# Loading the range flag into the engines' registers inside layer 1 of a two-layer graph kernel

## The chip, the cores and the metric

The kernel runs on one core of one Trainium2 chip. The metric is the device time of one execution in microseconds (us), lower is better. The core has five engines that run their own instruction queues: TensorE (PE in the profile, its weight loads apart as PEld), VectorE (DVE), ScalarE (ACT), GpSimd (POOL) and SyncE (SP, which here only issues DMAs).

## The reference

There are 3327 nodes with 64 features each, and a dense 3327 x 3327 adjacency matrix of zeros and ones. Two layers are added to `x`, each on `h = relu(layernorm(x))`. Cut to what matters:

```python
# layer 0: hyperbolic attention over the neighbours
c = 1.0 / r[0] ** 2
x_t = logmap0(h, c)
adj_att = sigmoid(left[:, None] + right[None, :] + b_att[0]) * adj    # left, right: x_t @ halves of w_att
x_local = logmap(h[:, None, :], h[None, :, :], c)                     # one vector per pair of nodes
support_t = einsum('ij,ijd->id', adj_att, x_local)
x = x + proj(expmap(h, support_t, c), c)
# layer 1: the last 100 neighbours of each row, weights halved from the last one backwards
mask = (adj != 0); rank = cumsum(mask, axis=1); deg = rank[:, -1:]
k = minimum(deg, 100); pos = rank - (deg - k)
w = mask * where(pos > 0, 0.5 ** (k - pos), 0.0)
x = x + w @ (relu(layernorm(x)) @ weight) + bias
```

## The kernel before

The nodes are padded to 26 blocks of 128. The program has two versions of the whole computation. `fast` (line 447) uses approximations that hold when the inputs lie in a certain range; while it runs it works out a one-element integer tile `flag` that is 0 when they do (`in_range`, lines 963 to 980, written by VectorE at line 979). `general` (line 86) computes the same without that assumption. `gnn_kernel` runs `fast`, loads `flag` into a register of each of the five engines (`values_load`, line 1367), and each engine branches on it (line 1368): `general` runs, and overwrites the output, only if the flag is above 0. For the inputs here it is 0, so every engine jumps over `general`'s instructions to the end of the program.

`fast` handles layer 0 in four strips of columns (8, 8, 6 and 4 blocks), each against all 26 row blocks in rounds. On the way it leaves, for each pair of nodes, a byte that says how many neighbours lie behind (`behind`), from which layer 1's weights are decoded. After a strip its per-node work (`post`, lines 992 to 1150) turns the sums into the new `x` and into `s2`, layer 1's input in two half-precision parts (written by ScalarE at line 1147 and by VectorE at line 1149).

Layer 1 starts at line 1271. It is a sum over the 26 row blocks: for a block `j`, `decode(j)` makes a weight tile `wt` of 128 x 3328, in turn on ScalarE (line 1285) and on VectorE (line 1287), and `add(j, wt, n)` (line 1299) multiplies `s2` of that block with one chunk of 512 columns, into one of seven accumulators `pw`. The loop over `order` does this for blocks 0 to 21. The last strip's blocks, 22 to 25 (`late` = 22 onwards), come after it, since their `s2` is ready only when the last strip's per-node work has ended. They are added chunk by chunk: the four late blocks into chunk `n`, then a copy of the accumulator to `ow` (lines 1340 and 1342, ScalarE and VectorE in turn), then, two chunks later, `close`: small matmuls with the layer's weight matrix (line 1328), the sum with `x_sb` on VectorE (line 1330), and the output DMA on SP (line 1332; the ragged end of the last block goes from ScalarE's queue, line 1334).

The order on TensorE, VectorE and ScalarE is the order of the source:

```python
IN_ORDER = {mybir.EngineType.PE, mybir.EngineType.DVE, mybir.EngineType.Activation}   # line 32
```

Layer 1 is recorded in `tc.manual_schedule(engines=IN_ORDER)` (line 1274). The instructions of POOL and SP are not in this set; the framework's scheduler sets their order. A weight load of TensorE is an instruction of its own ahead of its matmul, and carries the wait for `s2`.

Of the kernel before, what the change touches and what calls it, by code (L numbers as in the profile page):

```python
# [446 lines left out]
def fast(ctx, tc, x, adj_t, r, w_att, b_att, weight, bias, out, flag):  # L447

    nc = tc.nc
# [95 lines left out]
    def behind(j):  # L545
        if j in JD:
            return weight_of[:, j - JD.start]
        return behind_of["lo"][:, j] if j < JD.start else behind_hi[:, j - JD.stop]
# [619 lines left out]
    def per_node(k, pa):  # L1168
        nb = STRIPS[k][1]
        agg = post_pool.tile([P, nb, D + 1], F32, name="agg_last" if k + 1 == len(STRIPS) else "agg")  # L1170
        for c in range(0, nb, 4):
            m = min(4, nb - c)
            to, of = agg[:, c : c + m], pa[:, c * P : c * P + m * (D + 1)].rearrange("p (b d) -> p b d", b=m)
            if c == 0:
                V.tensor_copy(to, of)
            else:
                A.copy(to, of)
        return post(agg, k)
# [5 lines left out]
    def advance(portions):  # L1184
        for stage in stages:
            while portions > 0 and not stage.asked:
                portion = next(stage.portions, LATER)
                stage.asked = portion == ACT
                if portion >= LATER:
                    break  # L1190
                portions -= portion

    def asked_of_act():
        for stage in stages:
            if stage.asked:
                next(stage.portions)
                stage.asked = False

    def finish():
        for stage in stages:  # L1200
            for _ in stage.portions:
                pass
        stages.clear()
# [70 lines left out]
    with tc.tile_pool(name="l1", bufs=2, reuse_waits="tile") as l1, tc.manual_schedule(engines=IN_ORDER):  # L1274
        decoded = 0

        def decode(j):

            nonlocal decoded
            if j in JD:  # L1280
                return behind(j)
            wt = l1.tile([P, NP], U16, name="wt", bufs=7)
            decoded += 1
            if decoded % 2:
                A.activation(wt, behind(j), AF.Copy, scale=128.0)
            else:
                V.tensor_scalar(wt, behind(j), 128.0, None, op0=ALU.mult)  # L1287
            return wt

        every = [*order, *range(late, NB)]  # L1290
        weights = {j: decode(j) for j in every[: len(JD) + 1]}
        stages.append(Stage(per_node(len(STRIPS) - 1, pa)))
        sums.close()
        l1_ps = ctx.enter_context(tc.tile_pool(name="l1_ps", bufs=1, space=PSUM, reuse_waits="tile"))
        pw = [l1_ps.tile([P, f1 - f0], F32, name=f"pw{n}") for n, (f0, f1) in enumerate(chunks)]

        def add(j, wt, n):
            f0, f1 = chunks[n]
            T.matmul(pw[n], s2[:, j].rearrange("p c d -> p (c d)"), wt[:, f0:f1].bitcast(BF16),  # L1299
                     start=j == order[0], stop=j == NB - 1)  # L1300

        def bias(b0, nb):
            xb = x_sb[:, b0 : b0 + nb]
            G.tensor_add(xb, xb, bias_b[:, None, :].to_broadcast([P, nb, D]))  # L1304

        for i, j in enumerate(order):
            for jn in every[: i + 1 + LEAD]:
                if jn not in weights:
                    weights[jn] = decode(jn)
            asked_of_act()  # L1310
            advance(LAST)
            for n in range(len(chunks)):
                add(j, weights[j], n)
            if i % 4 == 3 and i < STRIPS[-2][0]:
                bias(i - 3, 4)
        finish()
        bias(STRIPS[-2][0], late - STRIPS[-2][0])
        bias(late, NB - late)
        for j in range(late, NB):
            if j not in weights:  # L1320
                weights[j] = decode(j)
        ow = [l1.tile([P, 512], F32, name="ow", bufs=4)[:, : f1 - f0] for f0, f1 in chunks]

        def close(n):
            f0, f1 = chunks[n]
            b0, nb = f0 // P, (f1 - f0) // P
            for b in range(nb):
                T.matmul(pw[n][:, b * D : (b + 1) * D], ow[n][:, b * P : (b + 1) * P], w2s, start=True, stop=True)
            o = l1.tile([P, 4, D], F32, name="o", bufs=4)
            V.tensor_add(o[:, :nb], pw[n][:, : nb * D].rearrange("p (b d) -> p b d", d=D), x_sb[:, b0 : b0 + nb])  # L1330
            full = nb if b0 + nb < NB else nb - 1
            nc.sync.dma_start(out[f0 : f0 + full * P, :].rearrange("(b p) d -> p b d", p=P), o[:, :full])
            if full < nb:
                nc.scalar.dma_start(out[f0 + full * P : N, :], o[: N - f0 - full * P, full])

        for n in range(len(chunks)):
            for j in range(late, NB):
                add(j, weights[j], n)
            if n % 2:
                A.copy(ow[n], pw[n])  # L1340
            else:
                V.tensor_copy(ow[n], pw[n])
            if n > 1:
                close(n - 2)
        close(len(chunks) - 2)
        close(len(chunks) - 1)


@with_exitstack
def gnn_kernel(  # L1350
    ctx: ExitStack,
    tc: tile.TileContext,
    x: bass.AP,
    adj_t: bass.AP,
    r: bass.AP,
    w_att: bass.AP,
    b_att: bass.AP,
    weight: bass.AP,
    bias: bass.AP,
    out: bass.AP,  # L1360
):
    keep = ctx.enter_context(tc.tile_pool(name="keep", bufs=1))
    flag = keep.tile([1, 1], I32, name="flag")
    args = (x, adj_t, r, w_att, b_att, weight, bias, out)
    with ExitStack() as inner:
        fast(inner, tc, *args, flag)
    cond = tc.nc.values_load(flag)
    with tc.If(cond > 0):
        with ExitStack() as inner:
            general(inner, tc, *args)  # L1370

# [27 lines left out]
```

## Time and profile before

| | |
|---|---|
| median of three runs | 416.37 us (414.42 to 418.77) |
| the profiled execution's own time | 418.25 us |
| its span (first to last instruction) | 416.4 us |
| VectorE, ScalarE, TensorE matmul busy | 90%, 88%, 87% |
| last computing instruction ends | 409.55 us after the span's start |

The profile is of one execution, and its times count from the first instruction. A line such as "L1299" is a line of the kernel before. A suffix q (SPq, DVEq) marks an engine's sequencer: register loads, branches, semaphore waits and DMA issues happen there and are not counted as the engine's busy time. In a timeline the first two numbers are start and duration, and the bracket at the end gives the idle time ahead of the instruction and what ended it.

### The profile page before, as it was taken

What the parts mean: (1) busy time and instruction counts of PE and PEld (TensorE: products, weight loads), DVE (VectorE), ACT (ScalarE), POOL (GpSimd) and SP (SyncE); (2) the same over time, 40 slices, a digit from 0 to 9 for tenths busy, and PEclk for the clock granted to TensorE, in tenths of its full rate; (3) what the DMA queues carried; (4) which work ended last, traced back from release to release, by engine and by line L of the source; (5) the groups of instructions that cost most, each with busy time, mean ns of one, the idle gap of its engine ahead of it and who ended that gap; (6) DMA issues with size and microseconds to landing.
All of it is one profiled execution on the core that took longest, in us unless ns stands there. A gap on an engine that the chain in (4) does not pass through costs nothing.

```text
span 416.4 us, 4699 instructions
## 1 busy us (share of the span) xinstructions
PE 361.1 (87%) x1436; PEld 154.4 (37%) x1460; DVE 373.1 (90%) x546; ACT 364.8 (88%) x411; POOL 124.0 (30%) x240
## 2 busy tenths in 40 slices
PE   0088999999997999999997999999777999899793
PEld 0063333333333333333333444444332333344352
DVE  4999799999999899999999798899989899898841
ACT  3589999999998899999999899999996999788810
POOL 8154200000000263930250163801405183452400
PEclk9998999999999899999999899999898999999987
DMA  7315544545466534554437255454643420000012
GB/s 218 123 40 143 161 148 147 158 145 161 146 186 181 152 107 148 153 151 109 145 113 178 94 153 151 119 146 128 186 117 104 114 87 0 2 0 0 2 25 65
DMA packets 23298, 48.99 MB, mean 118 GB/s; under 512 B 8789, under 2 KB 9245, under 8 KB 23265
## 3 DMA queue, kind: packets, MB, share of 16 engines
q1 hardware_dynamic: 20993, 47.66, 39.2%
q10 hardware_dynamic: 1808, 0.46, 0.6%
q0 software_dynamic: 464, 0.49, 0.5%
q8 instruction: 13, 0.21, 0.2%
q14 instruction: 20, 0.16, 0.1%
HBM read 46.40 MB, written 0.87 MB: 114 GB/s over the span
## 4 chain that ended last, share of the span: by engine, by line
DVE 33%; ACT 27%; PE 24%; issue 10%; POOL 3%; DMA 1%; DVEq 0%; POOLq 0%; ACTq 0%
DVE sg L663 9%; PE po L680 9%; ACT sg L653 8%; DVE sg L658 8%; ACT pq L857 8%; ACT pq L858 3%; DVE wt L1287 3%; PE pq L670 3%; PE pq L671 3%; DVE behind_lo L646 3%; PE pc L632 2%; PE pc L631 2%; ACT behind_lo L642 2%; ACT behind_hi L642 2%; PE pw L1299 2%
## 5 line engine op out<-in xcount | busy, mean ns | idle before, releaser
L680 PE MATMUL po<-sg,hw 128*65 128x512 f32 (+1 forms) x364 | 164.5, 576 | 0.5 <-DVE st L972 0.4
L663 DVE SCALAR_TENSOR_TENSOR sg<-pq,sg 128x1024 f32<-128x1024 f32 (+1 forms) x91 | 103.4, 1137 | 6.7 <-ACT pq L858 5.9
L658 DVE SCALAR_TENSOR_TENSOR sg<-sg,ad 128x1024 f32<-128x1024 f32 (+1 forms) x91 | 103.8, 1141 | 0.3
L653 ACT ACTIVATE sg<-left_b,right 128x1024 f32<-128x1024 f32 (+2 forms) x103 | 99.5, 979 | 0.0
L857 ACT ACTIVATE pq<-pq 128x1024 f32<-128x1024 f32 (+1 forms) x91 | 87.1, 957 | 3.5 <-PE pq L671 3.2
L858 ACT ACTIVATE pq<-pq 128x1024 f32<-128x1024 f32 (+1 forms) x91 | 86.2, 947 | 2.9
L680 PEld LDWEIGHTS po<-sg,hw 128*65 128x65 f32 x364 | 50.4, 141 | 71.3 <-issue 57.5
L631 PE MATMUL pc<-mask,ca 128*128 128x512 bf16 (+1 forms) x170 | 62.1, 365 | 11.1 <-DVE behind_hi L646 3.9
L670 PE MATMUL pq<-iu,ju 71*128 71x512 f16 (+1 forms) x182 | 68.2, 375 | 2.4 <-ACT jz L794 1.0
L671 PE MATMUL pq<-iz,jz 128*128 128x512 f16 (+1 forms) x182 | 67.2, 376 | 0.0
L632 PE MATMUL pc<-mask,cb 128*128 128x512 bf16 (+1 forms) x168 | 60.1, 368 | 2.2 <-ACT behind_lo L642 1.7
L620 DVE TENSOR_SCALAR mask<-ad 128x1024 bf16<-128x1024 f32 (+1 forms) x91 | 58.6, 645 | 0.0
L1044 POOL TENSOR_TENSOR dots<-dots,ih 128x8 f32<-128x8 f32 (+1 forms) x3 | 2.2, 720 | 134.3 <-DVE dots L1064 134.3
L1299 PE MATMUL pw<-wt,s 128*128 128x512 bf16 (+1 forms) x150 | 33.6, 374 | 4.3 <-DVE s L1149 2.2
L632 PEld LDWEIGHTS <-cb 128*128 128x128 bf16 x182 | 17.9, 98 | 51.7 <-issue 39.8
L631 PEld LDWEIGHTS <-ca 128*128 128x128 bf16 x175 | 17.3, 99 | 29.9 <-issue 17.8
L670 PEld LDWEIGHTS <-ju 71*128 71x128 f16 x182 | 18.1, 99 | 24.2 <-DVE sg L663 5.8
L1299 PEld LDWEIGHTS <-s 128*128 128x128 f16 x182 | 18.0, 100 | 23.6 <-issue 4.2
L642 ACT ACTIVATE behind_hi<-pc 128x1024 uint8<-128x1024 f32 (+2 forms) x25 | 21.8, 872 | 5.3 <-remote 3.3
L671 PEld LDWEIGHTS <-jz 128*128 128x128 f16 x182 | 18.2, 100 | 19.7 <-issue 3.3
L1304 POOL TENSOR_TENSOR x_sb<-x_sb,bias_b 128x256 f32<-128x256 f32 (+1 forms) x6 | 9.9, 1657 | 51.6 <-DVE w L1133 46.0
L642 ACT ACTIVATE behind_lo<-pc 128x1024 uint8<-128x1024 f32 (+2 forms) x29 | 24.9, 859 | 0.0
(313 smaller groups left out, 369.0 us busy)
## 6 DMA issues: line engine op xcount, KB each, us to landing
ad<-in_adj_t SPq DMA_DIRECT2D x65, 512.0 KB, 3.7
ad<-in_adj_t SPq DMA_DIRECT2D x26, 384.0 KB, 3.2
out<-o SPq DMA_DIRECT2D x6, 128.0 KB, 1.9
left_b<-left_d SPq DMA_DIRECT2D x1, 512.0 KB, 4.6
x_sb<-in_x ACTq DMA_DIRECT2D x1, 416.0 KB, 5.6
x_sb<-in_x SPq DMA_DIRECT2D x1, 416.0 KB
left_b<-left_d SPq DMA_DIRECT2D x1, 384.0 KB
jz<-iz POOLq DMA_DIRECT2D x2, 128.0 KB, 2.6
```

The source lines that it names most:

```text
L631: T.matmul(S.pc[:, f0:f1], ca, S.before[:, f0:f1], start=False, stop=True, skip_group_check=True)
L632: T.matmul(S.pc[:, f0:f1], cb, now[:, f0:f1], start=S.first, stop=True, skip_group_check=True)
L642: A.activation(kept, S.pc[:, : S.F], AF.Relu, scale=128.0 if j in JD else 1.0)
L653: A.activation(part(n, sg, j), S.left[:, : S.F], AF.Tanh, bias=right[:, j : j + 1], scale=0.5)
L658: V.scalar_tensor_tensor(sg, sg, 1.0, ad_of.pop(n)[:, :w], op0=ALU.add, op1=ALU.mult)
L663: V.scalar_tensor_tensor(sg, pq_of.pop(n)[:, :w], WD, sg, op0=ALU.add, op1=ALU.mult)
L670: T.matmul(part(n, pq, j, f0, f1), ju[:KB, j, :], S.iu[:, f0:f1], start=True, stop=False)
L671: T.matmul(part(n, pq, j, f0, f1), jz[:, j, :], S.iz[:, f0:f1], start=False, stop=True)
L680: T.matmul(S.po[: D + 1, f0:f1], hw[:, j, :], part(n, sg_of[n], j, f0, f1), start=j == NB - 1, stop=j == 0)
L857: A.activation(pq, pq, AF.Gelu, scale=-WG / QS)
L858: A.activation(pq, pq, AF.Gelu, scale=WH)
L1299: T.matmul(pw[n], s2[:, j].rearrange("p c d -> p (c d)"), wt[:, f0:f1].bitcast(BF16), start=j == order[0], stop=j == NB - 1)
```

## The change

The call that loads the flag into the registers moves from `gnn_kernel` into `fast`, ahead of the loop over the late blocks, and `fast` hands the loaded value back. The branch stays where it was.

```diff
@@ fast @@
             if full < nb:
                 nc.scalar.dma_start(out[f0 + full * P : N, :], o[: N - f0 - full * P, full])
 
+        general_too = nc.values_load(flag)
         for n in range(len(chunks)):
             for j in range(late, NB):
                 add(j, weights[j], n)
@@
         close(len(chunks) - 2)
         close(len(chunks) - 1)
+    return general_too
@@ gnn_kernel @@
     with ExitStack() as inner:
-        fast(inner, tc, *args, flag)
-    cond = tc.nc.values_load(flag)
-    with tc.If(cond > 0):
+        general_too = fast(inner, tc, *args, flag)
+    with tc.If(general_too > 0):
         with ExitStack() as inner:
             general(inner, tc, *args)
```

## The prediction

> **What bounds the kernel now.** I read the page's head first, then the chain that ended last, then the timeline around the place where the loads go, and last the flag's own line and the branch that follows it.
>
> ```profile
> PE 361.1 (87%) x1436; PEld 154.4 (37%) x1460; DVE 373.1 (90%) x546; ACT 364.8 (88%) x411; POOL 124.0 (30%) x240
> ```
>
> Three engines are near 90% busy, so anything put into their queues could cost. But the change touches only two short stretches: about 395 us, where the loads go, and the tail after 407 us, where they were. The chain of waits shows what sets the time there (start, duration, what):
>
> ```profile
> 395.04 1.81 DVE wt L1287
> ...
> 396.89 3.47 PE pw L1299 x9
> ...
> 409.26 0.29 DVE o L1330
> ```
>
> At 395 us the chain is on VectorE, which decodes the last block's weights; from 396.9 it is on TensorE; the last computing instruction is VectorE's `o`, which ends at 409.55. TensorE is waiting when the loads would come. The timeline (start, duration, instruction, idle time before it):
>
> ```profile
> 393.25 2.97 ACT L1285 ACTIVATE wt<-behind_hi 128x3328 uint16<-128x3328 uint8 x1
> 394.95 1.89 DVE L1287 TENSOR_SCALAR wt<-behind_hi 128x3328 uint16<-128x3328 uint8 x1
> 395.10 0.60 PE L1299 MATMUL pw<-wt,s 128*128 128x512 bf16 x2 [2.19 <-DVE s L1149]
> 396.27 0.38 PE L1299 MATMUL pw<-wt,s 128*128 128x512 bf16 x1 [0.57 <-ACT wt L1285]
> 396.89 2.61 PE L1299 MATMUL pw<-wt,s 128*128 128x512 bf16 x7 [0.25 <-DVE wt L1287]
> 397.31 0.69 DVE L1342 COPY ow<-pw 128x512 f32<-128x512 f32 x1 [0.47 <-PE pw L1299]
> 398.69 0.59 ACT L1340 COPY ow<-pw 128x512 f32<-128x512 f32 x1 [2.47 <-PE pw L1299]
> ```
>
> The flag's five loads, by its line (ns minimum/median/maximum, first and last start):
>
> ```profile
> L1367 POOLq TENSOR_LOAD <-flag x1: 497/497/497, 389.0 to 389.0; - x1
> L1367 PEldq TENSOR_LOAD <-flag x1: 486/486/486, 407.6 to 407.6; - x1
> L1367 DVEq TENSOR_LOAD <-flag x1: 542/542/542, 409.3 to 409.3; - x1
> L1367 ACTq TENSOR_LOAD <-flag x1: 911/911/911, 410.1 to 410.1; - x1
> L1367 SPq TENSOR_LOAD <-flag x1: 490/490/490, 410.9 to 410.9; - x1
> ```
>
> And the branch's line: the semaphore events are the first thing each engine does beyond it, so an engine's way across runs from its COMPARE_BRANCH to its EVENT_SEMAPHORE (first and last start before the semicolon).
>
> ```profile
> L1368 SPq EVENT_SEMAPHORE  x8: 17/17/17, 414.2 to 414.7; - x8
> L1368 DVEq COMPARE_BRANCH  x1: 72/72/72, 409.9 to 409.9; - x1
> L1368 ACTq COMPARE_BRANCH  x1: 54/54/54, 411.1 to 411.1; - x1
> L1368 SPq COMPARE_BRANCH  x1: 45/45/45, 411.4 to 411.4; - x1
> L1368 DVEq EVENT_SEMAPHORE  x1: 21/21/21, 412.9 to 412.9; - x1
> L1368 ACTq EVENT_SEMAPHORE  x1: 17/17/17, 413.8 to 413.8; - x1
> ```
>
> SP loads last (410.9), branches last (411.4) and comes out last (414.2); VectorE at 412.9, ScalarE at 413.8. After SP's eight waits (to 414.7) come the closing barriers, which end the span at 416.4. So SP sets the end; its slack over the next one, ScalarE, is 0.4 us.
>
> **What the Trainium skill says.** "DMA: Bandwidth & Descriptors", section "Latency and other measured facts", puts the floor of a `tensor_load` at about 600 ns; here four of the five took 0.49 to 0.54 us and ScalarE's 0.91, so the trace stands. "Runtime: NRT & Kernel Launch", section "Instruction fetch mechanics", says that a taken branch whose target isn't in the fetched pages stalls the engine for a DMA fetch; the trace agrees: 411.4 to 414.2 on SP is 2.7 us for a branch of 45 ns, 3.0 on VectorE, 2.7 on ScalarE. That stall needs the branch, not the load, and stays where the branch stays. "TensorE: Matmul & The Clock Gate", Part 1, gives a window of 3.413 us in which an idle TensorE is set to half clock; the windows view has 0.51 granted from 397.4 to 400.9, right after the wait above, so it is already paid once.
>
> **The change part by part.**
>
> *Where the loads land.* The built instruction order differs in only three places. On TensorE the load now stands between the weight load of block 22 (which waits for `s2` from L1149) and its first matmul; on VectorE after the last decode, ahead of the first `ow` copy; on ScalarE after its last decode, ahead of its first `ow` copy. On POOL and SP nothing moves: POOL's load already ran at 389.0, behind its last `rn_last`, and SP's is still behind all seven output DMAs. These two engines aren't in the order written by hand (IN_ORDER), so the new source line doesn't place them. No instruction is added, removed or made to wait longer: the load waits for VectorE's write of `flag`, which ran at 357.9, 37 us earlier. No DMA is issued by the move.
>
> *VectorE.* At the old place the load began at 409.3, just as the last `o` did (409.26 to 409.55), so a load runs beside the instruction ahead of it. Now it begins at about 394.97 and ends at 395.5, under a decode that runs to 396.84; the next copy starts at 397.31. Cost 0; without the decode it would be 0.54.
>
> *ScalarE.* It begins at about 393.3, under the decode that ends at 396.22, and the next copy is at 398.69. Even at 0.91 us: cost 0.
>
> *TensorE.* Here the load stands behind a wait, and what is queued behind it is the whole of the late sums. The old load ran at 407.6, just after VectorE's last `ow` copy (timeline: 407.08 + 0.42 = 407.50) had released the last matmuls ahead of it, with some matmuls still to execute: it passes when the wait ahead of it is met. So it begins at 395.09 and the two matmuls of 395.10 slip to about 395.6. They are done being issued before 396.27, where the third matmul waits for ScalarE's decode in any case, and 396.89, where the fourth waits for VectorE's. The pair may slip some 0.7 us before the third moves, and some 1.2 before the fourth does; 0.49 fits the first and 0.91 the second. Cost 0. Bounds: 0 if the load is passed during the wait, +0.55 if its cover is gone.
>
> *The tail.* TensorE's branch comes 0.5 us earlier, VectorE's 0.6, ScalarE's 1.0. None of them ends last, so directly this is worth 0: SP still issues its last DMA (it starts at 409.8), loads for 0.49, branches, and fetches for 2.7. What can be gained is relief. SP's output DMAs by their line (ns minimum/median/maximum, first and last start), and the last one in the DMA view (its last column: us from issue to landing):
>
> ```profile
> L1332 SPq DMA_DIRECT2D out<-o x7: 372/372/1019, 402.0 to 409.8; - x7
> out<-o SPq DMA_DIRECT2D x1, 32.0 KB, 4.1
> ```
>
> The last issue takes 1.02 us where the median is 0.37 (the timeline has SP's issues end at 410.8), and ScalarE's load, which is removed from there, lies across it (410.1 to 411.0). But ScalarE's own output DMA (in the timeline 409.59, 0.51) lies there too and stays. Upper bound of the gain: 1.02 - 0.37 = 0.65; lower bound 0; on the loss side, nothing excludes a later fetch on SP when the others' fetches move beside its DMA issue, so +0.2, the spread of the fetches above (2.7 to 3.0) rounded down. I take a gain of 0.2, about a third of the bound, as ScalarE's DMA by itself explains 0.3 of it. Past SP there is little anyway: the last output lands 4.1 us after its issue at 409.8, at 413.9, and SP waits for it between 414.2 and 414.7, so 0.3 to 0.8 us earlier SP would wait for the landing.
>
> *Sum.* The profiled execution took 418.25 us: its span of 416.40 and 1.85 around it. 0 + 0 + 0 - 0.2 gives 418.05. That execution was 1.9 above the median of the runs (416.37; 414.42 to 418.77), which are spread wider than any term here; the same -0.2 on the median gives 416.2.
>
> **The rivals.**
>
> *A, the forecast:* hidden in front, SP last at the end: 416.2. Chance 0.65.
>
> *B, relief in full:* ScalarE's load was what held SP's last issue, and the end comes 0.65 us earlier: 415.7. For it: the overlap of the two. Against: other DMA work lies there too, and the landing soon takes over. Chance 0.20.
>
> *C, the load stalls TensorE:* one mechanism, at TensorE's queue at 395.1. The load holds the late sums until past 396.9, and the thinner activity costs TensorE a second stretch at half clock. It decides from a slip of over 1.2 us at that place. Price: 0.5 for the load, and half of a stretch of 3.4 us, 1.7; +2.2, 418.6. For it: the half-clock stretch already follows this wait. Against: the load fits into a wait that is there. Chance 0.12.
>
> *D, SP's load goes ahead also,* as the change's words would have it: its 0.49 and 0.07 to the branch leave the end: -0.56, 415.8. Against: SP's instruction order. Chance 0.03.
>
> **How the numbers follow.** The likeliest case gives 416.2. The cases reach from 415.7 to 418.6, and a median of a few runs may fall about 2 us either side of its value, as the three shown do: 414.1 to 418.7. A measurement of this kernel tells about 1% (4.2 us) from no change; no case reaches it. Faster by over 1%: 0.02; slower: 0.03, a stall at TensorE with a cost beyond C's; within: 0.95.
>
> **What would show it.** Right: three loads at about 393.3, 395.0 and 395.1, SP's still near 411, POOL's near 389; the fourth late matmul still released by VectorE's `wt`; the copies at 397.3 and 398.7 unmoved; SP's branch again the last. B: an SP issue near 0.4 instead of 1.0. C: TensorE waiting for "issue" before the fourth matmul, and low clock over more than 3.5 us after 397. Wrong altogether: a difference that sits before 390 us, where no instruction moves.

## The result and the profile after

The changed kernel takes 416.75 us (median of 20 runs, 415.34 to 420.84) against 416.67 of the kernel before (median of 20, 414.42 to 419.08): ratio 1.0006, interval 0.9984 to 1.0028. That is no difference that can be measured. The profiled execution took 418.75 us with a span of 416.7.

The loads stand where the instruction order puts them. The flag's loads by their line (which is now 1336; ns minimum/median/maximum, first and last start):

```profile
L1336 POOLq TENSOR_LOAD <-flag x1: 499/499/499, 388.4 to 388.4; - x1
L1336 ACTq TENSOR_LOAD <-flag x1: 468/468/468, 392.5 to 392.5; - x1
L1336 DVEq TENSOR_LOAD <-flag x1: 545/545/545, 392.8 to 392.8; - x1
L1336 PEldq TENSOR_LOAD <-flag x1: 487/487/487, 394.5 to 394.5; - x1
L1336 SPq TENSOR_LOAD <-flag x1: 1005/1005/1005, 410.4 to 410.4; - x1
```

SP's load is still behind the output DMAs, and it takes 1.0 us where it took 0.49. The timeline around the early loads:

```profile
394.38 1.89 DVE L1287 TENSOR_SCALAR wt<-behind_hi 128x3328 uint16<-128x3328 uint8 x1
394.51 0.10 PEld L1299 LDWEIGHTS <-s 128*128 128x128 f16 x1 [2.58 <-DVE s L1149]
395.02 1.05 PE L1299 MATMUL pw<-wt,s 128*128 128x512 bf16 x3 [2.70 <-DVE s L1149]
396.32 3.65 PE L1299 MATMUL pw<-wt,s 128*128 128x512 bf16 x9 [0.25 <-DVE wt L1287]
396.73 0.69 DVE L1343 COPY ow<-pw 128x512 f32<-128x512 f32 x1 [0.47 <-PE pw L1299]
```

Seen from the weight load, the first matmul comes 0.51 us later (394.51 to 395.02; before it was 395.09 to 395.10), and TensorE still waits 0.25 us for VectorE's decode ahead of the fourth. The decode ends at 396.27 and the chain's last piece is this:

```profile
408.69 0.29 DVE o L1330
```

From the decode's end to the end of that `o` it is 408.98 - 396.27 = 12.71 us; before it was 409.55 - 396.84 = 12.71. So in front the loads cost nothing. That everything here is 0.57 us earlier than before comes from ahead of 390 us and is no effect: `flag` was written at 357.9 in one execution of the kernel before, at 355.9 in another, and at 357.3 here, and from the end of that write to the end of the last decode it is 38.8 us in all three.

Behind the last `o` it looks different. The branch's line (now 1369), and SP's output DMAs:

```profile
L1369 SPq EVENT_SEMAPHORE  x8: 17/17/17, 414.5 to 415.0; - x8
L1369 PEldq COMPARE_BRANCH  x1: 3831/3831/3831, 407.0 to 407.0; - x1
L1369 ACTq COMPARE_BRANCH  x1: 54/54/54, 409.6 to 409.6; - x1
L1369 SPq COMPARE_BRANCH  x1: 45/45/45, 411.4 to 411.4; - x1
L1369 ACTq EVENT_SEMAPHORE  x1: 17/17/17, 412.3 to 412.3; - x1
L1332 SPq DMA_DIRECT2D out<-o x7: 372/384/1009, 401.4 to 409.9; - x7
```

ScalarE branches 1.5 us earlier than before (1.0 counted from the last `o`) and is beyond the branch at 412.3; SP, which sets the end, branches at 411.4 as before, though the last `o` ended 0.57 us earlier, and is beyond it at 414.5. One SP issue is again 1.0 us long. From the end of the last `o` to the end of the span, called the tail below, it is 7.74 us; before it was 416.40 - 409.55 = 6.85.

### The profile page after: what moved, and what is told of

It is laid out like the page before. It is cut to its first block, busy times and chain, and to the rows that moved or that the text cites. A ratio compares the mean times of both kernels' runs of the same rounds, so it can differ in the third digit from the quotient of the medians.

```text
span 416.7 us, 4699 instructions
## 1 busy us (share of the span) xinstructions
PE 356.8 (86%) x1436; PEld 152.0 (36%) x1460; DVE 373.1 (90%) x546; ACT 364.7 (88%) x411; POOL 124.0 (30%) x240
## 3 DMA queue, kind: packets, MB, share of 16 engines
q1 hardware_dynamic: 20993, 47.66, 38.8%
## 4 chain that ended last, share of the span: by engine, by line
DVE 39%; ACT 23%; PE 21%; issue 10%; POOL 3%; DMA 1%; DVEq 0%; POOLq 0%; ACTq 0%
DVE sg L663 11%; DVE sg L658 10%; PE po L680 8%; ACT pq L857 7%; ACT sg L653 6%; DVE behind_lo L646 3%; ACT pq L858 3%; DVE wt L1287 3%; PE pq L670 3%; PE pq L671 2%; PE pc L631 2%; PE pc L632 2%; DVE behind_hi L646 2%; ACT behind_lo L642 2%; PE pw L1299 2%
## 5 line engine op out<-in xcount | busy, mean ns | idle before, releaser
L680 PE MATMUL po<-sg,hw 128*65 128x512 f32 (+1 forms) x364 | 161.4, 567 | 0.5 <-DVE st L972 0.4
L671 PE MATMUL pq<-iz,jz 128*128 128x512 f16 (+1 forms) x182 | 66.2, 371 | 0.0
```

Of the source, the lines that this page charges most:

```text
L671: T.matmul(part(n, pq, j, f0, f1), jz[:, j, :], S.iz[:, f0:f1], start=False, stop=True)
L680: T.matmul(S.po[: D + 1, f0:f1], hw[:, j, :], part(n, sg_of[n], j, f0, f1), start=j == NB - 1, stop=j == 0)
```

## The experiments

All ratios are to the kernel before. The loads and waits in front are told by times counted from the decode's end, the rest by times counted from the end of the last `o`. A tail is that of one profiled execution; an interval belongs to the ratio alone.

**A second look at both kernels.** No edit.

> The changed kernel, once more, for a second look at its tail. Theory 1 (SP's path sets the end; its long output issue comes from the overlap with ScalarE's own output DMA issue): ratio 0.998 to 1.002; again one SP issue near 1.0 us that overlaps ScalarE's issue, SP's load after its last issue, and SP beyond the branch 1.5 to 2.5 us after ScalarE; from the end of the last o to the end of the span 6.8 to 7.7 us. Rival (ScalarE's load was what stretched SP's issue, and the profile shown was an accident): no SP issue over 0.6 us, tail below 6.5 us.

> The kernel before, once more, for a second look at its tail. Theory 1 (TensorE's fetch of instructions beyond its branch stretches what SP issues beside it; the load that the change moves off TensorE brings that fetch 0.5 us earlier, onto SP's last issue but one): from the end of the last o to the end of the span 6.6 to 7.1 us, SP's last issue but one 0.37 us, the last near 1.0. Rival (the difference of the tails is chance from one execution to the next): between 6.5 and 7.8 us, with either issue long.

The changed kernel: ratio 1.0003 (0.9981 to 1.0025), tail 7.59. The kernel before: tail 6.97, one run of 416.37 us. The two tails of each lie 0.12 and 0.15 apart, and between the kernels are 0.6 to 0.9 us. In the kernel before it is SP's last issue that is long, in the changed kernel the last but one (0.81 us the second time; the last then took 0.79).

**SP's load early too.** The one load that the change left in the tail is placed like the others: SP is added to the engines whose order in layer 1 is the source's.

```diff
-    with ..., tc.manual_schedule(engines=IN_ORDER):
+    with ..., tc.manual_schedule(engines=IN_ORDER | {mybir.EngineType.SP}):
```

> The changed kernel with SP added to the engines whose order is the source's in layer 1, so that SP's load also comes ahead of the output DMAs. Theory 1: SP branches straight after its last issue, and the tail from the end of the last o to the end of the span becomes 0.5 to 1.0 us shorter than with the changed kernel, 6.0 to 7.0 us; the whole time by 0.1 to 0.25 percent, too little for the timing to tell. Rival (the landing of the last output sets the end): SP is beyond its branch earlier but then waits at its first eight events, which spread over more than 0.8 us, and the tail stays within 0.2 us.

> The kernel with SP's load ahead of the output DMAs, once more, since its first interval only just left no change. Theory 1 (SP's own sequence after the last o sets the end, and its load is the one that counts): tail 5.9 to 6.4 us again, ratio 0.995 to 0.999. Rival (the first result was chance): ratio 0.999 to 1.002 and a tail near 6.9.

Ratio 0.9972 (0.9948 to 0.9997), the second time 0.9976 (0.9958 to 0.9995); tails 6.13 and 6.00. Its lines of the first:

```profile
L1336 SPq TENSOR_LOAD <-flag x1: 483/483/483, 357.3 to 357.3; - x1
L1369 SPq COMPARE_BRANCH  x1: 45/45/45, 409.6 to 409.6; - x1
L1369 SPq EVENT_SEMAPHORE  x8: 17/17/17, 412.5 to 413.0; - x8
```

The last `o` ends at 408.57, so SP branches 1.0 us after it instead of 2.5. The timing tells it from no change both times; ahead of the first I had not expected that. SP's own sequence sets the end, not the landing of the last output, but it is close: the landing came 3.92 us after the last `o`, and SP, beyond the branch at 3.90, asks for it among the waits that follow, which take 0.1 us or less each (the second time 3.81 and 3.77).

**The ragged end from SP's queue.** This takes ScalarE's output DMA away from beside SP's.

```diff
-                nc.scalar.dma_start(out[f0 + full * P : N, :], o[...])
+                nc.sync.dma_start(out[f0 + full * P : N, :], o[...])
```

> The changed kernel with the ragged end of the output sent from SP's queue instead of ScalarE's. Theory 1: with no issue on ScalarE beside SP's, no SP issue is over 0.6 us; SP has one more issue of 0.4 to 0.5 us, so it branches 0.2 us earlier to 0.2 us later than with the changed kernel, measured from the end of the last o; time the same within 0.3 percent. Rival (the long issue comes from the output queue being full or from fetches of instructions): one SP issue stays near 1.0 us, and SP branches 0.4 us or more later.

```profile
L1332 SPq DMA_DIRECT2D out<-o x7: 372/384/925, 403.8 to 412.2; - x7
L1334 SPq DMA_DIRECT2D out<-o x1: 287/287/287, 413.0 to 413.0; - x1
```

Ratio 1.0020 (0.9991 to 1.0049), tail 7.71. An issue of 0.93 us stays with nothing on ScalarE beside it, and the next is 0.76; SP branches only 0.1 us later than with the changed kernel, not 0.4 or more as the rival had it. So the theory that ScalarE's DMA stretches SP's issue falls.

**No branch at all.** `general` and the branch are left out; nothing reads the flag, and its register loads are gone from the trace too.

> The changed kernel without the branch and without the general version behind it; the flag is computed and never read. Theory 1: SP loses its load (0.5 to 1.0), its branch and its fetch (2.7 to 3.0), and waits only for the landing of the last output; the tail becomes 1 to 2.5 us shorter, the time 0.2 to 0.6 percent. Rival (the landing sets the end already): tail shorter by less than 0.5 us.

```profile
L1332 SPq DMA_DIRECT2D out<-o x7: 372/373/449, 397.9 to 405.7; - x7
```

Ratio 0.9952 (0.9929 to 0.9975), tail 5.45. No SP issue is over 0.45 us, although ScalarE's issue (0.51) is there as ever. With the last experiment this leaves the branches and what they fetch as what stretches SP's issue: the changed kernel's early loads are long over by then, and SP's own comes behind the stretched issue. Here the landing does set the end: SP has done all else by 1.04 us and goes on at 4.20, just after the last output has landed (4.19). So of the 6.85 us before, about 1.4 is what can be saved on SP's way out, unless the output itself lands earlier.

**TensorE's load apart.** A helper joins the registers of two loads, one early, one at the program's end; in the first kernel TensorE alone is late, in the second TensorE alone is early. In the diff, `early` and `late` stand for the lists of engines.

```diff
-        general_too = nc.values_load(flag)
+        general_too = nc.values_load(flag, engines=early)
...
+    general_too = both_of(general_too, tc.nc.values_load(flag, engines=late))
```

> The changed kernel, but with TensorE's load left at the end as before; the loads of VectorE and ScalarE are still early. Theory 1: TensorE's branch is again 1.4 us before the end of the last o instead of 2.0, SP's last issue but one is 0.37 us again, and the tail goes back to 6.5 to 7.1 us from the 7.6 to 7.7 of the changed kernel. Rival 1 (the earlier branches of VectorE and ScalarE do it): the tail stays at 7.5 to 7.8. Rival 2 (chance): anything between. Time within 0.3 percent of before for all.

> The kernel before with TensorE's load alone moved to the change's place. Theory 1: SP's last issue but one is stretched to 0.8 to 1.0 us and the tail is 7.3 to 7.8 us. Rival 1 (VectorE's and ScalarE's branches do it): SP's last issue but one 0.37 us and a tail of 6.6 to 7.1. Rival 2 (chance): anything between. In front, TensorE's first two late matmuls start 0.5 us after the weight load they follow, the third and fourth where they did. Time within 0.3 percent of before for all.

TensorE late, then TensorE alone early, SP's issues:

```profile
L1332 SPq DMA_DIRECT2D out<-o x7: 372/372/1635, 400.4 to 408.2; - x7
L1332 SPq DMA_DIRECT2D out<-o x7: 372/383/830, 399.8 to 408.1; - x7
```

The first (last start 408.2, the last `o` ended at 407.92) has the long issue last, as before; in the second it is the last but one, as in the changed kernel. TensorE's load decides which issue is hit. The rest of the expectation failed: with TensorE late the tail is 8.25 us, not 6.5 to 7.1 (ratio 0.9996, 0.9973 to 1.0019), and with TensorE alone early 7.33 (1.0023, 0.9997 to 1.0049). The 8.25 can hardly be typical of that kernel's runs: 1.3 to 1.4 us more than before would be a ratio of 1.003, which lies outside the interval.

**SP early, TensorE late.** Both edits.

> Loads of SP, VectorE and ScalarE early (SP's ahead of the output DMAs), TensorE's at the end as before. Theory 1: the tail is 0.2 to 0.5 us shorter than the 6.1 us with all loads early, since SP's last issue but one is 0.37 us again; ratio to before 0.994 to 0.998. Rival 1 (TensorE's fetch is not what stretches SP's issue): tail 6.1 us or more. Rival 2 (the gain of SP's early load was chance): ratio 0.999 to 1.002.

Ratio 1.0000 (0.9969 to 1.0031), tail 6.87, the last issue 1.56 us. The last but one is 0.37 again, as theory 1 had it, but its shorter tail did not come: the last is held instead, and for longer. The tail is the one that rival 1 forecast, though not for its reason, since the stretch did move with TensorE's branch.

**More loads in front.** Three more at the same place, or one ahead of each of chunks 1 to 6, both with SP's load early.

```diff
         general_too = nc.values_load(flag)
+        for _ in range(3):
+            general_too = general_too + nc.values_load(flag)
```

```diff
         for n in range(len(chunks)):
+            if n:
+                general_too = general_too + nc.values_load(flag)
             for j in range(late, NB):
```

> As the kernel with SP's load early, with three more loads of the flag on every engine at the same place; the branch tests the sum of the four. Theory 1 (TensorE's load is covered by a wait of 1.2 us, and nothing else covers it): on TensorE four loads take 2.0 to 2.3 us after block 22's weight load, and the fourth late matmul starts 0.8 to 1.1 us after VectorE's last decode instead of 0.05; VectorE's and ScalarE's loads stay hidden; time 1 us longer than with SP's load early, ratio to before 0.998 to 1.002. Rival (TensorE passes the loads while it waits for s2, so that any number is free): fourth matmul 0.05 us after the decode as before.

> As the kernel with SP's load early, with one more load of the flag on every engine ahead of each of the chunks 1 to 6 of the late sums, where TensorE is on the chain; the branch tests the sum. Theory 1 (it is the wait that makes the load free, not the load): each costs up to 0.55 us on the chain from the fourth late matmul to the last o, which takes 14 to 16 us instead of 12.7; time 1.3 to 3.3 us longer than with SP's load early. Rival (a load runs beside the matmuls queued ahead of it, so it is free anywhere): the chain takes 12.7 to 13.2 us.

With four loads in the place of one:

```profile
394.10 0.10 PEld L1299 LDWEIGHTS <-s 128*128 128x128 f16 x1 [2.58 <-DVE s L1149]
395.83 3.58 PE L1299 MATMUL pw<-wt,s 128*128 128x512 bf16 x9 [3.92 <-issue]
```

The first matmul comes 1.73 us after the weight load (the three more take 0.31 us each, not 0.49), and the idle time ahead of it is put down to issue. The decode ended at 395.85, and the fourth matmul starts 0.80 us later instead of 0.06. From the decode to the last `o` it is 13.31 us, 0.6 more; ratio 1.0002 (0.9973 to 1.0032), against 0.9972 and 0.9976 without the three. So the slack is there; it is 1.0 us (1.73 less the 0.74 by which the fourth slipped), near the predicted 1.2. With a load ahead of each chunk the stretch is 12.83 us instead of 12.72: six loads of 0.30 us on TensorE, on its chain, cost 0.1. (It is compared with executions in which TensorE's half-clock stretch of 3.4 us lies wholly behind the decode, as it does here; seven of them took 12.71 to 12.73. Where the stretch begins ahead of the decode's end, as in the first run with SP's load early, it is 12.4 to 12.5.) Theory 1 fell there and the rival stands: here a load runs while the matmuls queued ahead of it execute. Ratio 0.9988 (0.9968 to 1.0007). The tail is 7.08, about 1 us longer than with SP's load early alone: TensorE branches 0.3 us later, and SP's last issue but one takes 1.28 us.

**More loads at the end.** Three more on every engine, SP's included.

```diff
         general_too = fast(inner, tc, *args, flag)
+    for _ in range(3):
+        general_too = general_too + tc.nc.values_load(flag)
```

> The changed kernel with three more loads of the flag on every engine at the program's end; the branch tests the sum of the four. Theory 1 (SP's sequence sets the end): SP's four loads take 2.2 to 3 us and the tail grows to 8.8 to 9.8 us from 7.6 to 7.7; the other engines' loads cost nothing, though TensorE's branch now comes 1.7 us later and no longer stretches SP's issues (0.37 to 0.45 each); ratio to before 1.002 to 1.007. Rival (the landing of the last output sets the end): tail longer by 0.3 us at most.

```profile
L1332 SPq DMA_DIRECT2D out<-o x7: 372/373/655, 401.9 to 409.7; - x7
```

Tail 7.68, ratio 1.0009 (0.9979 to 1.0039): no longer than the changed kernel's. The number is the rival's, its reason is not: SP is beyond the branch at 5.47 us and the last output landed at 4.46. SP's four loads take 1.7 us together, but TensorE's branch is now 1.5 us later, and the long issue and the long first load are gone (last two issues 0.37 and 0.66, load 0.59). So the collision seems to have been worth about as much as the three loads; this is one execution.

**All tails together,** worked out from the traces, in us from the end of the last `o`. TensorE's fetch is taken to be the first 16 KB instruction packet that queue q8 moves there: it begins 1.0 to 1.1 us after TensorE's branch in every kernel that branches, and without the branch q8 moves none in the tail (11 packets in all, 13 in the kernel before).

| kernel | TensorE branches | its fetch ends | long SP issue, its end | SP's load takes | SP branches | tail |
|---|---|---|---|---|---|---|
| before | -1.39 | 0.88 | last, 1.27 | 0.49 | 1.89 | 6.85 |
| before, again | -1.36 | 1.15 | last, 1.52 | 0.49 | 2.14 | 6.97 |
| changed | -1.99 | 0.36 | last but one, 0.78 | 1.01 | 2.46 | 7.74 |
| changed, again | -1.99 | 0.11 | last but one, 0.58 | 0.86 | 2.47 | 7.59 |
| TensorE alone early | -1.99 | 0.18 | last but one, 0.60 | 1.18 | 2.46 | 7.33 |
| TensorE alone late | -1.40 | 1.41 | last, 1.89 | 0.50 | 2.50 | 8.25 |
| ragged end from SP | -1.99 | 0.17 | last but one, 0.70 | 0.56 | 2.58 | 7.71 |
| SP early | -1.99 | 0.06 | last but one, 0.44 | early | 1.04 | 6.13 |
| SP early, again | -1.99 | 0.19 | last but one, 0.59 | early | 1.19 | 6.00 |
| SP early, TensorE late | -1.39 | 1.34 | last, 1.80 | early | 1.85 | 6.87 |
| four loads, SP early | -1.84 | 0.15 | last but one, 0.54 | early | 1.39 | 6.34 |
| chunk loads, SP early | -1.67 | 0.62 | last but one, 1.05 | early | 2.27 | 7.08 |
| end loads | -0.48 | 1.94 | last, 0.91 | 0.59 | 2.91 | 7.68 |
| no branch | none | none | none | none | none | 5.45 |

In all rows but the last two the held issue ends 0.4 to 0.5 us after TensorE's fetch. That moving TensorE's branch moves the stretch is shown; that the fetch is what holds SP is inferred from this, and "end loads" does not fit it, since its issue ends before the fetch does. The other fetches beside it, 8 KB packets on queue q14, are not what holds it: in the four executions with SP's and TensorE's loads both early none is under way during the long issue. SP's load is 0.9 to 1.2 us long in three executions with an early TensorE load (changed, changed again, TensorE alone early) and 0.56 in a fourth. In the three it begins at 1.38, 1.53 and 1.21, and ends at 2.39 in each; so it seems to wait for something that comes at a fixed time after the last `o`; what that is stays open.

## Why the prediction was right, and where it was not

*The whole.* 416.2 was forecast and 416.75 measured, inside the range, and no change was the likeliest. The hit says little by itself: the range of 414.1 to 418.7 is far wider than any term of the sum and holds cases B and D too. The forecast's gain of 0.2 us is 0.05%, the measured ratio 1.0006 with 0.22% on either side; the timing decides neither. It tells more than the prediction allowed, though: not 1% but 0.24 to 0.28% was told from no change, with SP's load early.

*The loads in front.* Right in each term. TensorE's load ran when the weight load ahead of it was released; the first two matmuls slipped 0.5 us, the third and fourth not at all; VectorE's copy and the decodes kept their distances. ScalarE's first copy came 2.04 us after the decode's end instead of 1.85, but it lies inside the half-clock stretch and goes with that stretch's start: 1.77 and 1.85 in the two executions of the kernel before, 2.04 and 1.85 in the two of the changed one, and from the fourth copy on they agree to 0.01. Two small errors: ScalarE's and VectorE's loads came even earlier than I said, up to 1.6 us before the decode ahead of them started, so here these two run ahead of an instruction that is still queued. And "+0.55 if its cover is gone" was too high for a single load elsewhere: six loads on the chain cost 0.1 us in all.

*SP sets the end, and its load is not moved.* Right, and the reason that the change does nothing of use. Case D, against which the order spoke, became true when SP was added to that order. I had priced it at 0.56; the tails shrink by 0.7 to 1.0 against the kernel before, and the time by 0.24 to 0.28% (1.0 to 1.2 us, with the intervals above).

*The relief in the tail.* This is the step that failed: "I take a gain of 0.2". Its bounds were a gain of 0.65 and a loss of 0.2, and the tails are 0.6 to 0.9 longer. I read the overlap of ScalarE's load with SP's long issue as a cause. With ScalarE's load gone and TensorE's left late that issue took 1.64 us, so case B falls; and the 0.3 that ScalarE's DMA was to explain falls with the ragged end on SP's queue, where the issue stayed long. What the edit does is the reverse: TensorE's branch comes 0.6 us earlier, the stretch moves from SP's last issue to the last but one, SP's last issue so ends no earlier (1.33 us after the last `o`, before 1.27; the second time 1.48 and 1.52), and SP's load then takes 0.4 to 0.5 us more. I had the term in the sum, as a later fetch on SP, but sized it by the spread of fetches in a profile where they did not meet. The intervals of the time allow the loss in the tail and do not show it.

*Case C* fell: no wait for "issue" ahead of the fourth matmul, and the half-clock stretch after the wait was 3.4 us once, as before. But that the stretch is the price of this wait, as the prediction took it, is not shown. In the execution without the branch TensorE waits there as long (2.58 us ahead of the weight load, as in the others) and has the full clock from 316.6 to 408.8 us. In the other 13 executions the stretch begins 78.5 us after the end of the one before it, at 315 to 321 us; what decides it stays open.

*"Wrong altogether: a difference that sits before 390 us"* was a bad sign to choose: executions of one kernel differ there by 2 us.

## What to carry to other kernels

Before pricing a move out of a program's tail, ask which engine leaves last and whether the move touches that engine: four of five loads moved or already lay early, and the one that counted stayed, since a scheduler and not the source places it. In these runs a register load was all but free where instructions were queued ahead of it (six for 0.1 us), and cost something only behind a wait that had drained the queue, once they outlasted that wait's slack (four for 0.6 us). An engine that reaches a far branch earlier fetched earlier here, so look at what its fetch then meets.

## What the runs showed of the hardware that was not expected

The way over the second version costs about 0.5% (ratio 0.9952 without it, 2 us; 1.0 to 3.0 by the interval, and 1.4 to 1.5 by the tails), although on each engine it is one register load and a branch, whose own record is 0.05 to 0.07 us on all but TensorE. From SP's branch to its next instruction it is 2.6 to 3.5 us. In front, behind a first load of 0.47 to 0.55 us, further loads take 0.27 to 0.31; in the busy tail, up to 0.44. The spread of the runs goes with TensorE's granted clock: among the 20 runs of the changed kernel the shortest spans are 413.4 and 413.5 us at mean clocks of 0.986 and 0.987, and those at 0.968 or less are 416.9 to 418.7; one stretch at half clock, in the late sums, accounts for 1.7 us (12.71 us with it from the decode to the last `o`, 11.04 in the execution without the branch, in which TensorE had the full clock there).
